# Four graph layers on one core: layer 1 folds W1 W2 ahead of the adjacency, the next pair's norm (in layer 3 its scores too) is issued half a pair ahead, attention weights are 1024 nodes wide

## Chip, core and metric

The kernel runs on one core of one Trainium2 chip. The metric is device time in microseconds (us). "Ratio" always means the mean time of one kernel's fast runs over that of the other's in the same rounds, with a 95% interval, so it is not quite the ratio of the two medians that are quoted.

## The reference, cut to what matters

x is [8, 2048, 64] in fp32, adj is [2048, 2048]. Each of four layers is `x = x + layer(relu(layernorm(x)))`.

```python
# layer 0: T0 = h, T1 = A h, T2 = 2 A (A h) - h; weights per node, w_n = sum_d embedding[n,d] weight[d]
# layer 1
v = h with row 0 replaced by intervention_value
for _ in range(3):
    effects = adj @ v                                  # per batch
    v = relu([v, effects] @ W1.T + b1) @ W2.T + b2
# layer 2: adj @ h, a scale and bias per channel, a linear map
# layer 3: graph attention
e   = leaky_relu(s1[:, None] + s2[None, :], 0.2)       # s1 = h @ a1, s2 = h @ a2
att = softmax(where(adj > 0.5, e, -9e15))
out = elu(att @ h)
```

## The kernel before

Two batches (a "pair") are worked on at a time, so every layer has four pairs. adj lies transposed in SBUF for the whole run. A product with it takes node-major data (128 nodes by 16 chunks by 128 channels) as the stationary operand and gives blocks of 512 nodes, feature-major. The tile framework gives each tile a buffer in program order ("two `blkb` tiles" means that the third waits until the first has been read), and then a scheduler sets the order on each engine. In the traces a ready instruction waits behind the one ahead of it in that order: in the kernel before, a weight on VectorE, for which TensorE then waited 0.75 us, began at 2306.29 us, behind an elu operation that had waited 1.26 us for GpSimd (both rows stand in the prediction).

The norm ahead of each layer. Its squares lie in `blkb`.

```python
    def norm_relu(xt, name):
        h = node_tile(f"h_{name}")
        mean = small.tile([P, G2], F32, name="mean")
        nc.vector.tensor_reduce(mean, groups(xt), axis=AX.X, op=ALU.add)
        ...                                             # h = x - mean
        for q in range(4):
            sq = blk("blkb", f"sq_{name}_{q}")
            nc.scalar.activation(sq, h[:, 4 * q:4 * q + 4, :]..., AF.Square)
            nc.vector.tensor_reduce(var[:, 8 * q:8 * q + 8], sq..., axis=AX.X, op=ALU.add)
        ...
        nc.gpsimd.tensor_tensor(rstd, var, mhalf, op=ALU.pow)
        nc.vector.scalar_tensor_tensor(groups(h), groups(h), 0.0, spread(rstd, C), op0=ALU.max, op1=ALU.mult)
```

Layer 1, the step that is done 3 times 4 blocks for each pair.

```python
                ps = adj_mm(v, nb, f"1_{p}_{s}")                     # 16 matmuls of 512
                eT = blk("blka", f"eT_{nm}")
                nc.vector.tensor_copy(eT, ps)
                ph = bank("tr", f"ph_{nm}")
                nc.tensor.matmul(ph, later["w1v"], vT[:, cols], start=True, stop=False)
                nc.tensor.matmul(ph, later["w1e"], eT, start=False, stop=True)
                hT = blk("blkb", f"hT_{nm}")
                nc.scalar.activation(hT, ph, AF.Relu, bias=later["b1"])
                pn = back_to_nodes(hT, later["w2"], nm)              # 4 matmuls of 128: "bn"
                ...
                if not last:
                    nc.vector.tensor_tensor(v_new[:, js, :], pn, ..., op=ALU.add)
                    pv = bank("tr", f"pv_{nm}")
                    nc.tensor.matmul(pv, later["w2"], hT, start=True, stop=True)
                    nc.scalar.activation(vT[:, cols], pv, AF.Identity, bias=later["b2"])
```

Layer 3 for each pair: scores with their products on VectorE, then per batch and block of 512 nodes 16 weights and 16 products on TensorE; then the elu, partly on GpSimd.

```python
                for j in range(NCH):
                    w = l3p.tile([P, 512], F32, name="w", bufs=3)
                    nc.vector.scalar_tensor_tensor(w, Grow[:, nb * 512:(nb + 1) * 512], R[:, j, bb:bb + 1],
                                                   adjT[nb][:, j, :], op0=ALU.max, op1=ALU.mult)
                    nc.tensor.matmul(acc[:C + 1, :], he[:, j, :], w, start=(j == 0), stop=(j == NCH - 1))
```

The loop around it issues a pair's norm when the pair begins:

```python
        for p in range(NP):
            xt = x_next
            h = norm_relu(xt, f"{layer}_{p}")
            ...
            attention(p, xt, h, l3p, ones)
```

Of the kernel before, what the change touches and what calls it, by code (L numbers as in the profile page):

```python
# [18 lines left out]
# Exponent shifts of the attention weights, see attention().  # L19
# [4 lines left out]
def kernel(  # L24
# [19 lines left out]
    """Four residual layers over one graph, two batches ("a pair") at a time.  # L44

    Two layouts of a pair's [node, batch, channel] values are used:
    node-major    [128 nodes, 16 node chunks, 2 batches x 64 channels] and
    feature-major [2 batches x 64 channels, 2048 nodes].
    adj is transposed once and stays in SBUF; a product with it takes a node-major
    operand (stationary) and gives a feature-major result.  # L50
    """
# [17 lines left out]
    adjT = [adjp.tile([P, NCH, 512], F32, name=f"adjT{nb}") for nb in range(NB)]  # L69
# [48 lines left out]
    def norm_relu(xt, name):  # L118
        """relu(layernorm(x)), node-major; mean and variance over each node's 64 channels."""
        h = node_tile(f"h_{name}")  # L120
# [3 lines left out]
        nc.vector.tensor_tensor(groups(h), groups(xt), spread(mean, C), op=ALU.subtract)  # L124
        var = small.tile([P, G2], F32, name="var")
        for q in range(4):
            sq = blk("blkb", f"sq_{name}_{q}")
            nc.scalar.activation(sq, h[:, 4 * q:4 * q + 4, :].rearrange("p j f -> p (j f)"), AF.Square)
            nc.vector.tensor_reduce(
                var[:, 8 * q:8 * q + 8], sq.rearrange("p (g c) -> p g c", c=C), axis=AX.X, op=ALU.add  # L130
            )
# [4 lines left out]
            groups(h), groups(h), 0.0, spread(rstd, C), op0=ALU.max, op1=ALU.mult  # L136
# [3 lines left out]
    def adj_mm(v, nb, name):  # L140
        """[2 x 64 channels, 512 nodes] of adj @ v, in PSUM."""
        ps = bank("mm", f"av_{name}_{nb}")
        for m in range(NCH):
            nc.tensor.matmul(ps, v[:, m, :], adjT[nb][:, m, :], start=(m == 0), stop=(m == NCH - 1))  # L144
        return ps
# [20 lines left out]
    def load_adj(nb):  # L166
        for t in range(4):
            r0 = nb * 512 + t * P
            for q in range(4):
# [5 lines left out]
                dst = adjT[nb][:, 4 * q:4 * q + 4, t * P:(t + 1) * P]  # L175
# [8 lines left out]
    # L0 weights, [input channel (on both partition halves), k, (d, output channel)]  # L184
# [7 lines left out]
    # embedding @ bias, node-major  # L192
# [17 lines left out]
    def two_halves(src, width, name):  # L210
        t = consts.tile([P, width], F32, name=name)
        for hf in range(2):
            nc.sync.dma_start(t[hf * C:(hf + 1) * C, :], src)
        return t

    def row(src, reps, name):
        """64 values of a DRAM vector, `reps` times over, on every partition."""
        t = consts.tile([P, reps, C], F32, name=name)
        nc.sync.dma_start(t, bass.AP(tensor=src.tensor, offset=src.offset, ap=[[0, P], [0, reps], [1, C]]))
        return t  # L220

    def block_diag_T(src, name):
        """[[src.T, 0], [0, src.T]] of a [64, 64] DRAM matrix."""
# [5 lines left out]
        t = consts.tile([P, P], F32, name=name)  # L229
# [8 lines left out]
    def load_later():  # L238
# [3 lines left out]
        later["wo"] = block_diag_T(w_out, "wod")  # L242
        later["b1"] = two_halves(b1[:, None], 1, "b1c")
        later["b2"] = two_halves(b2[:, None], 1, "b2c")
        later["bnl"] = two_halves(b_nl[:, None], 1, "bnl")
        later["b2r"] = row(b2, 2, "b2r")
        later["bor"] = row(b_out, 2, "bor")
        later["a1"] = row(a[:C, 0], 1, "a1r")
        later["a2"] = row(a[C:, 0], 1, "a2r")
        wn = two_halves(w_nl, 2, "wnl")  # L250
        ws = consts.tile([P, 1], F32, name="wsum")
        nc.vector.tensor_scalar(wn, wn, INV_SQRT2, None, op0=ALU.mult)
        nc.vector.tensor_tensor(ws, wn[:, 0:1], wn[:, 1:2], op=ALU.add)
        later["wsum"] = ws
# [6 lines left out]
    def layer0(p, xt, h):  # L261
# [23 lines left out]
        for nb in range(NB):  # L285
            ps = adj_mm(t1, nb, f"{nm}b")
            t2T = blk("blka", f"t2T_{p}_{nb}")
            nc.vector.scalar_tensor_tensor(  # L288
                t2T, ps, 2.0, t0T[:, nb * 512:(nb + 1) * 512], op0=ALU.mult, op1=ALU.subtract
            )  # L290
# [21 lines left out]
    def back_to_nodes(fT, wmat, name):  # L312
        """fT [2 x 64, 512 nodes] through a block-diagonal weight: node-major, in PSUM."""
# [12 lines left out]
    def layer1(p, xt, v):  # L326
        steps = 3
        nc.scalar.copy(v[0:1, 0, :], later["iv"])
        vT = to_feat(v, f"1_{p}")
        add_row(xt, later["b2r"])  # L330
        for s in range(steps):
            last = s == steps - 1
            v_new = None if last else node_tile(f"v_{p}_{s}")
            for nb in range(NB):
                nm = f"1_{p}_{s}_{nb}"
                cols = slice(nb * 512, (nb + 1) * 512)
                ps = adj_mm(v, nb, f"1_{p}_{s}")
                eT = blk("blka", f"eT_{nm}")
                nc.vector.tensor_copy(eT, ps)  # L339
                ph = bank("tr", f"ph_{nm}")  # L340
                nc.tensor.matmul(ph, later["w1v"], vT[:, cols], start=True, stop=False)  # L341
                nc.tensor.matmul(ph, later["w1e"], eT, start=False, stop=True)  # L342
                hT = blk("blkb", f"hT_{nm}")
                nc.scalar.activation(hT, ph, AF.Relu, bias=later["b1"])  # L344
                pn = back_to_nodes(hT, later["w2"], nm)
# [3 lines left out]
                else:  # L349
                    f = later["b2r"].rearrange("p b c -> p (b c)")  # L350
                    nc.vector.tensor_tensor(
                        v_new[:, js, :], pn, f[:, None, :].to_broadcast([P, 4, 2 * C]), op=ALU.add
                    )
                    pv = bank("tr", f"pv_{nm}")
                    nc.tensor.matmul(pv, later["w2"], hT, start=True, stop=True)
                    nc.scalar.activation(vT[:, cols], pv, AF.Identity, bias=later["b2"])
            v = v_new

# [1 line left out]
    def layer2(p, xt, h):  # L360
        add_row(xt, later["bor"])
        for nb in range(NB):
            ps = adj_mm(h, nb, f"2_{p}")
            gT = blk("blka", f"gT_{p}_{nb}")
# [5 lines left out]
    def make_mask():  # L370
        for nb in range(NB):
            for q in range(4):
                m = adjT[nb][:, 4 * q:4 * q + 4, :]
                nc.vector.tensor_scalar(m, m, THRESHOLD, None, op0=ALU.is_gt)

# [1 line left out]
    # With z = s1_i + s2_j, exp(leaky_relu(z)) = max(exp(z), exp(0.2 z))  # L377
    #   = exp(0.2 s1_i) exp(s2_j) max(exp(0.8 s1_i), exp(-0.8 s2_j)),
    # and the factor of i alone cancels in the softmax. With S = max_j s2_j, the three factors
    # are scaled to  # L380
    #   e_j = exp(s2_j - S + QE), G_i = exp(0.8 (s1_i + S) - KR), R_j = exp(0.8 (S - s2_j) - KR).
    # G_i is capped at exp(CAP): above every R_j it is a factor of i alone again. All stay in
    # range for any s1 and for S - s2_j up to 132; |h| <= 8 after the layer norm bounds it by
    # 8 sqrt(2) |a2|.
    # A row without neighbours is a softmax over equal values: the mean of all h_j.
    def attention(p, xt, h, l3p, ones):
        s1 = l3p.tile([P, NCH, 2], F32, name="s1", bufs=1)
        s2 = l3p.tile([P, NCH, 2], F32, name="s2", bufs=1)
        for s, ar in ((s1, later["a1"]), (s2, later["a2"])):
            flat = s.rearrange("p j b -> p (j b)")  # L390
            for q in range(4):
                tmp = blk("blkb", f"hs_{p}_{q}")
                tg = tmp.rearrange("p (g c) -> p g c", c=C)
                nc.vector.tensor_tensor(
                    tg, groups(h)[:, 8 * q:8 * q + 8, :], ar.to_broadcast([P, 8, C]), op=ALU.mult
                )
                nc.vector.tensor_reduce(flat[:, 8 * q:8 * q + 8], tg, axis=AX.X, op=ALU.add)
        # S of each batch, on every partition
# [13 lines left out]
        G = l3p.tile([P, NCH, 2], F32, name="G", bufs=1)  # L412
# [7 lines left out]
        # sum of h over the nodes, on every partition  # L420
        pS = bank("tr", f"pS_{p}")
        for j in range(NCH):
            nc.tensor.matmul(pS[:, :2 * C], ones, h[:, j, :], start=(j == 0), stop=(j == NCH - 1))
        hsum = l3p.tile([P, 2 * C], F32, name="hsum", bufs=1)
        nc.vector.tensor_copy(hsum, pS[:, :2 * C])

        for bb in range(2):
            bs = slice(bb * C, (bb + 1) * C)
            Grow = feat_tile(f"Grow_{p}_{bb}")
            for nb in range(NB):  # L430
                pg = bank("tr", f"pg_{p}_{bb}_{nb}")
                for t in range(4):
                    nc.tensor.transpose(
                        pg[:, t * P:(t + 1) * P],
                        G[:, 4 * nb + t, bb:bb + 1].to_broadcast([P, P]), ident,
                    )
                nc.scalar.copy(Grow[:, nb * 512:(nb + 1) * 512], pg)  # L437
            he = l3p.tile([P, NCH, C + 1], F32, name="he")
            nc.vector.tensor_tensor(
                he[:, :, :C], h[:, :, bs], E[:, :, bb:bb + 1].to_broadcast([P, NCH, C]), op=ALU.mult  # L440
            )
            nc.scalar.copy(he[:, :, C:], E[:, :, bb:bb + 1])
            for nb in range(NB):
                nm = f"{p}_{bb}_{nb}"
                acc = bank("mm", f"acc_{nm}")
                for j in range(NCH):
                    w = l3p.tile([P, 512], F32, name="w", bufs=3)
# [96 lines left out]
```

## Time and profile before

| before | |
|---|---|
| time | 2748.63 us median of 3 runs (2747.21 to 2751.48) |
| layer 0, 1, 2, 3 | 979, 896, 243, 627 us |
| TensorE idle in them | 97, 48, 2, 120 us |
| TensorE busy, whole run | 90% of the span |

The lengths are cut at the layers' first products in the trace.

### The profile page before, as it was taken

The numbers are of one execution on the slowest core, as the hardware profiler recorded it, in microseconds if no ns is written. First come the engines' busy times: TensorE is split into PE (matmuls) and PEld (weight loads), VectorE is DVE, ScalarE is ACT, GpSimd is POOL, SyncE is SP. The second block draws the span as 40 slices with busy tenths as digits, with TensorE's granted clock in tenths as the row PEclk, the third lists the DMA queues.
The fourth block names the chain that finished last, engine by engine and source line by source line (L and its number), as shares of the span: only waits on it lengthen the run. The fifth ranks groups of instructions, "written<-read, shape, count | busy, mean of one in ns | idle before, by whom it ended". The sixth has DMA issues, their size and how long they took to land.

```text
span 2745.0 us, 18187 instructions
## 1 busy us (share of the span) xinstructions
PE 2478.4 (90%) x7296; PEld 1075.3 (39%) x7296; DVE 1160.1 (42%) x2245; ACT 219.2 (8%) x393; POOL 177.7 (6%) x138
## 2 busy tenths in 40 slices
PE   5889999999999999989989989998999977959697
PEld 3444444443443444434434434443444223222232
DVE  3135626626526530110110111012227878878787
ACT  1110010010000000010010000001001110111110
POOL 0000000000000000000000000001000120111111
PEclk7999999999999999999999999999999998979899
DMA  6310000010000000000000000000001010000000
GB/s 135 123 48 1 19 13 1 1 31 1 0 31 1 0 31 0 0 31 0 0 31 0 0 22 9 0 0 31 31 31 61 2 30 1 8 23 8 8 1 16
DMA packets 40873, 53.55 MB, mean 20 GB/s; under 512 B 28500, under 2 KB 28500, under 8 KB 37716
## 3 DMA queue, kind: packets, MB, share of 16 engines
q1 hardware_dynamic: 37908, 35.60, 4.5%
q0 software_dynamic: 2880, 16.78, 1.8%
q8 instruction: 58, 0.95, 0.1%
q14 instruction: 27, 0.22, 0.0%
HBM read 35.59 MB, written 16.78 MB: 19 GB/s over the span
## 4 chain that ended last, share of the span: by engine, by line
PE 57%; issue 23%; DVE 13%; POOL 5%; ACT 1%; DMA 1%; SPq 0%; POOLq 0%; DVEq 0%; ACTq 0%
PE av L144 32%; DVE x L307 10%; PE y L300 3%; PE bn L316 3%; POOL rstd L134 2%; PE av_2a L144 2%; PE av_3a L144 2%; PE av_1a L144 2%; PE ph L342 2%; PE av_3b L144 2%; PE av_2b L144 2%; PE av_1b L144 2%; PE av_0b L144 2%; PE ph L341 2%; POOL yx L476 1%
## 5 line engine op out<-in xcount | busy, mean ns | idle before, releaser
L452 PE MATMUL acc<-w,he 128*65 128x512 f32 x1024 | 459.8, 597 | 21.4 <-DVE w L448 21.0
L144 PE MATMUL av<-adjT,h 128*128 128x512 f32 x1024 | 452.2, 598 | 11.0 <-DVE h L135 11.0
L144 PE MATMUL av<-adjT,v 128*128 128x512 f32 x1024 | 449.9, 592 | 0.0
L448 DVE SCALAR_TENSOR_TENSOR w<-Grow,R,adjT 128x512 f32<-128x512 f32 x512 | 380.2, 758 | 37.4 <-ACT Grow L437 12.0
L307 DVE SCALAR_TENSOR_TENSOR x<-y,emb,x 128x128 f32<-128x128 f32 x1024 | 355.0, 350 | 69.8 <-PE y L300 31.0
L144 PEld LDWEIGHTS av<-adjT,h 128*128 128x128 f32 x1024 | 195.3, 192 | 249.3 <-issue 238.1
L339 DVE COPY eT<-av 128x512 f32<-128x512 f32 x48 | 33.2, 692 | 607.9 <-PE av L144 607.9
L144 PEld LDWEIGHTS av<-adjT,v 128*128 128x128 f32 x1024 | 193.6, 190 | 239.2 <-issue 239.2
L452 PEld LDWEIGHTS acc<-w,he 128*65 128x65 f32 x1024 | 129.0, 137 | 323.1 <-DVE w L448 208.8
L300 PE MATMUL y<-wt,T 64*128 64x512 f32 x512 | 144.2, 635 | 35.9 <-DVE x L307 32.3
L300 PE MATMUL y<-wt,t2T 64*128 64x512 f32 x512 | 135.2, 594 | 8.9 <-DVE t2T L288 8.9
L300 PE MATMUL y<-wt,t1T 64*128 64x512 f32 x512 | 134.4, 591 | 0.0
L134 POOL TENSOR_TENSOR rstd<-var,mhalf 128x32 f32<-128x32 f32 x16 | 87.2, 5451 | 454.1 <-DVE var L132 453.9
L105 POOL DMA_DIRECT2D xs<-x x12 | 7.2, 602 | 1586.5 <-DVE x L348 859.8
L300 PEld LDWEIGHTS y<-wt,T 64*128 64x128 f32 x512 | 43.3, 187 | 132.4 <-PE y L300 104.2
L275 DVE COPY t<-t 128x512 f32<-128x512 f32 x16 | 11.1, 691 | 195.3 <-PE t L274 195.3
L344 ACT ACTIVATE hT<-ph,b1c 128x512 f32<-128x512 f32 x48 | 33.0, 687 | 707.2 <-PE ph L342 693.0
L300 PEld LDWEIGHTS y<-wt,t2T 64*128 64x128 f32 x512 | 55.1, 188 | 65.0 <-issue 53.4
L174 PE MATMUL adjt<-ident,adj 128*128 128x128 f32 x256 | 48.3, 334 | 33.6 <-DMA adj<-in_adj_dram 31.7
L300 PEld LDWEIGHTS y<-wt,t1T 64*128 64x128 f32 x512 | 55.5, 188 | 55.6 <-issue 55.6
L135 DVE SCALAR_TENSOR_TENSOR h<-h,rstd 128x2048 f32<-128x2048 f32 x16 | 36.7, 2292 | 89.9 <-POOL rstd L134 89.9
L402 PE MATMUL pm<-ident,mx 128*2 128x128 f32 x4 | 1.4, 346 | 78.4 <-DVE mx L400 78.4
(134 smaller groups left out, 1823.0 us busy)
## 6 DMA issues: line engine op xcount, KB each, us to landing
adj<-in_adj_dram SPq DMA_DIRECT2D x64, 256.0 KB, 3.7
xs<-x POOLq DMA_DIRECT2D x12, 1024.0 KB, 4.2
x<-xs SPq DMA_DIRECT2D x12, 1024.0 KB, 4.8
x<-in_x_dram SPq DMA_DIRECT2D x8, 512.0 KB, 6.5
out_dram<-x POOLq DMA_DIRECT2D x8, 512.0 KB, 4.8
wt<-in_L_gnn_weight_dram SPq DMA_DIRECT2D x6, 256.0 KB, 6.8
emb<-in_L_gnn_embedding_dram SPq DMA_DIRECT2D x1, 128.0 KB, 5.7
b2r<-in_L_gnn_b_dram SPq DMA_DIRECT2D x1, 64.0 KB, 5.6
```

What stands on the lines that cost most here:

```text
L134: nc.gpsimd.tensor_tensor(rstd, var, mhalf, op=ALU.pow)
L135: nc.vector.scalar_tensor_tensor(groups(h), groups(h), 0.0, spread(rstd, C), op0=ALU.max, op1=ALU.mult)
L144: nc.tensor.matmul(ps, v[:, m, :], adjT[nb][:, m, :], start=(m == 0), stop=(m == NCH - 1))
L174: nc.tensor.transpose(ps[:, m * P:(m + 1) * P], st[:, m * P:(m + 1) * P], ident)
L300: nc.tensor.matmul(y[:, bb, :], terms[k][hs, :], wt[hs, k, dg * 512:(dg + 1) * 512], start=(k == 0), stop=(k == K - 1),)
L307: nc.vector.scalar_tensor_tensor(xj, y[:, :, d * C:(d + 1) * C], emb[:, j, e:e + 1], xj, op0=ALU.mult, op1=ALU.add,)
L316: nc.tensor.matmul(ps[:, t, :], fT[:, t * P:(t + 1) * P], wmat, start=True, stop=True)
L339: nc.vector.tensor_copy(eT, ps)
L341: nc.tensor.matmul(ph, later["w1v"], vT[:, cols], start=True, stop=False)
L342: nc.tensor.matmul(ph, later["w1e"], eT, start=False, stop=True)
L448: nc.vector.scalar_tensor_tensor(w, Grow[:, nb * 512:(nb + 1) * 512], R[:, j, bb:bb + 1], adjT[nb][:, j, :], op0=ALU.max, op1=ALU.mult,)
L452: nc.tensor.matmul(acc[:C + 1, :], he[:, j, :], w, start=(j == 0), stop=(j == NCH - 1))
```

## The change

Its intent: fewer matmuls in layer 1; norms and scores hidden behind the pair before; fewer VectorE instructions in layer 3. `hook()` issues the next pair's norm, and in layer 3 its scores too; in layers 0 to 2 it stands at the second of a pair's four blocks (layer 2's is cut here). The diff, cut to its core:

```diff
 # layer 1: u = W1e v goes through adj, W1 W2 is one matrix, relu's result in a feature tile
+        for nb in range(NB):
+            pn = back_to_nodes(gT[:, nb * 512:(nb + 1) * 512], later["w1e"], f"u_{p}_{nb}")
+            nc.vector.tensor_copy(u[:, 4 * nb:4 * nb + 4, :], pn)
...
-                ps = adj_mm(v, nb, f"1_{p}_{s}")
-                eT = blk("blka", f"eT_{nm}")
-                nc.vector.tensor_copy(eT, ps)
-                ...                                         # ph: two matmuls
-                hT = blk("blkb", f"hT_{nm}")
-                nc.scalar.activation(hT, ph, AF.Relu, bias=later["b1"])
-                pn = back_to_nodes(hT, later["w2"], nm)
+                nc.tensor.matmul(ps, later["w1v2" if s else "w1v"], gT[:, cols], start=True, stop=False)
+                for m in range(NCH):
+                    nc.tensor.matmul(ps, u[:, m, :], adjT[:, nb, m, :], start=False, stop=(m == NCH - 1))
+                nc.scalar.activation(gT_new[:, cols], ps, AF.Relu, bias=later["b1s" if s else "b1"])
+                if last and nb == 1:
+                    hook()                                  # the next pair's norm
+                pn = back_to_nodes(gT_new[:, cols], later["w2" if last else "w1e2"], nm)
-                    pv = bank("tr", f"pv_{nm}")             # and its copy
 # layer 0: T2's factor and difference go into the weights
-            nc.vector.scalar_tensor_tensor(t2T, ps, 2.0, t0T[...], op0=ALU.mult, op1=ALU.subtract)
+            nc.scalar.copy(t2T, ps)
+            if nb == 1:
+                hook()
 # layer 3: weights of 1024, score products on GpSimd, elu's -1 taken from x beforehand
-                nc.vector.tensor_tensor(tg, groups(h)[:, 8 * q:8 * q + 8, :], ar..., op=ALU.mult)
+                nc.gpsimd.tensor_tensor(tg, hg[:, 8 * q:8 * q + 8, :], ar..., op=ALU.mult)
...
+        nc.gpsimd.tensor_scalar(xt, xt, -1.0, None, op0=ALU.add)
...
+                    w = w2j[:, j % 2]                       # two tiles of two weights: four in all
+                    nc.vector.scalar_tensor_tensor(w, Grow, R[:, j, bb:bb + 1],
+                                                   adjT[:, 2 * n2:2 * n2 + 2, j, :], op0=ALU.max, op1=ALU.mult)
+                    for t in range(2):
+                        nc.tensor.matmul(acc[:C + 1, t, :], h[:, j, bb, :], w[:, t, :], ...)
+                    if bb == 0 and n2 == 1 and j == 0:
+                        hook()                              # the next pair's norm and scores
```

A "half" below is one batch and 1024 nodes in layer 3: 32 products on TensorE, four halves to a pair. The second half of a pair carries the hook.

## The prediction

> **What bounds the kernel now.** I read the busy time per stretch first, cut at the layer boundaries that the chain of waits shows, then the groups by shape, the chain of waits inside layer 1, and two stretches of the timeline. The first view gives, for each layer, its length and then the busy time of TensorE, weight loads, VectorE, ScalarE and GpSimd, the granted clock and the DMA.
>
> ```profile
> 0.00:979.00 979.00, 882.51 (x3002) 403.20 (x3003) 462.75 (x1156) 50.57 (x86) 29.89 (x14) 0.97 0.10 28
> 979.00:1875.00 896.00, 847.65 (x2236) 386.94 (x2234) 116.51 (x145) 74.21 (x115) 24.73 (x9) 0.97 0.03 12
> 1875.00:2118.00 243.00, 241.47 (x641) 111.50 (x641) 84.13 (x89) 21.96 (x32) 23.57 (x7) 0.99 0.07 26
> 2118.00:2745.00 627.00, 506.73 (x1421) 173.67 (x1419) 496.67 (x858) 72.42 (x160) 99.55 (x108) 0.92 0.05 14
> ```
>
> TensorE is busy 95% of layer 1 and 99% of layer 2: there only fewer matmuls or a shorter gap helps. In layer 3 it idles 120 us while VectorE is busy 79%: neither is full, so they wait for each other. Layer 0 idles 97 us, mostly while adj loads and where VectorE works off the per-node sums.
>
> The chain inside layer 1 (start, us, what) gives the period of one 512-node block in steps 1 and 2, 17.64 us:
>
> ```profile
> 1047.76 1.05 PE ph L342 x2
> 1049.67 1.14 PE bn L316 x8
> 1050.81 0.86 PE pv L355 x2
> 1051.66 12.88 PE av L144 x30
> ```
>
> An fp32 matmul is two instructions; 30 in 12.88 us make 0.858 us per matmul of 512 columns. The block is 18 of them (16 of adj, two of W1), a "bn" of 1.16 us, and "pv", 0.86. The last step has no pv and takes 16.78.
>
> At a pair's end the timeline shows what TensorE waits for:
>
> ```profile
> 1417.20 5.45 POOL L134 TENSOR_TENSOR rstd<-var,mhalf 128x32 f32<-128x32 f32 x1 [1.58 <-DVE var L132]
> 1422.69 2.29 DVE L135 SCALAR_TENSOR_TENSOR h<-h,rstd 128x2048 f32<-128x2048 f32 x1 [5.64 <-POOL rstd L134]
> 1425.37 3.76 PE L152 MATMUL tf<-ident,h 128*128 128x128 f32 x16 [11.36 <-ACT h L328]
> ```
>
> The norm of the next pair ends in the open: 11.4 us idle, and a pair comes every 225 us. In layer 2, and at most pairs of layer 0, the norm is already under matmuls.
>
> Layer 3 has blocks of 15.3 us (8 per pair) and, once per pair, a gap: pairs repeat every 162 us, 8 x 15.3 = 122.5 of them blocks. The gap is norm, scores and weights in a row on VectorE:
>
> ```profile
> 2262.52 2.29 DVE L135 SCALAR_TENSOR_TENSOR h<-h,rstd 128x2048 f32<-128x2048 f32 x1 [5.58 <-POOL rstd L134]
> 2264.85 1.29 DVE L394 TENSOR_TENSOR hs<-h,a1r 128x512 f32<-128x512 f32 x2
> 2274.42 2.27 DVE L122 TENSOR_REDUCE mean<-x 128x32 f32<-128x2048 f32 x1
> 2280.97 2.36 DVE L439 TENSOR_TENSOR he<-h,E 128x1024 f32<-128x1024 f32 x2
> 2286.76 13.22 DVE L448 SCALAR_TENSOR_TENSOR w<-Grow,R,adjT 128x512 f32<-128x512 f32 x16 [0.76 <-ACT Grow L437]
> 2303.91 0.91 DVE L448 SCALAR_TENSOR_TENSOR w<-Grow,R,adjT 128x512 f32<-128x512 f32 x1
> 2304.35 1.01 POOL L476 TENSOR_TENSOR yx<-yx,o 128x256 f32<-128x256 f32 x1
> 2306.08 0.29 DVE L479 TENSOR_SCALAR yx<-yx 128x256 f32<-128x256 f32 x1 [1.26 <-POOL yx L477]
> 2306.29 0.75 DVE L448 SCALAR_TENSOR_TENSOR w<-Grow,R,adjT 128x512 f32<-128x512 f32 x1
> ```
>
> The last four rows show the wait that will matter: the next weight stands behind an elu operation that waits for GpSimd.
>
> [...] (692 for N=512; he, 1222 for 1024), and the weight in the groups view is 758, somewhat over. Back to back, starts are closer than durations: 0.66 us for a weight of 512 (2306.29 to 2306.95). So I take 1.2 us for one of 1024. [...] the GpSimd add beside a weight took 1.01 us, without one 0.69, and that weight 0.91 instead of 0.75. [...]
>
> **Layer 1.** Since v = W2 g + b2, the change sends u = W1e v through adj and folds W1 W2. One pass then needs 16 adj matmuls and one more in the same PSUM bank; the copy eT, the second W1 matmul and pv go. A block becomes 17 x 0.858 + 1.16 = 15.75, plus about 0.1: in the order of instructions one 0.86 matmul covers the relu (0.69 plus latency, 0.95). 48 x 15.85 = 761. Each pair adds to_feat 3.76 and u = W1e v, four times 1.16 = 4.64: 8.4, with a small wait 9, so 36. Its norm is issued in the last step and the order shows it finished under matmuls. Sum 797 for 896: **-99**, less 2 where VectorE still drains layer 0's sums: -97.
>
> **Layer 0.** T2 is folded into the weights; t2T becomes a ScalarE copy, and no longer stands behind the norm on VectorE. Before, TensorE waited for it 2.96 us in pairs 1 to 3 (8.9 in all). The per-node sums stay: 0.384 us each (61 in 23.42 us), 3.07 per tile of 8, above TensorE's 2.85. **-8**. The two operations on wt (about 2 us) fall where VectorE is idle.
>
> **Layer 2.** The same matmuls, no gap to close: 0.
>
> **Layer 3.** TensorE per half (1024 nodes, one batch): 32 x 0.858 = 27.4 plus transposes of the result 1.2. VectorE: 16 weights x 1.2 = 19.2 instead of 32 x 0.66 = 21.1, and the elu loses two operations. So a half is bound by TensorE once started. But the order puts both blocks' elu in one run on VectorE, behind four weights (two tiles are all the buffers). Six GpSimd operations (0.61 to 0.7, 4.6 us in all) and two exps stand in it. Counting from the end of the half before: weights 2 and 3 by 2.5 us, divisor by 4, GpSimd by 7, elu by 8.4, weight 4 by 9.7; TensorE has used up four by 8.1. It loses 1.6: **30.3 per half**. Where the transposes of G stand behind the half before (second half of the next pairs, and third) no weight is ahead; the first comes at 4.9 and the second at 10.3, then 15 x 1.72: **36**.
>
> The half that carries the next pair's norm and scores: weights alternate with this work. VectorE in order waits for squares (their two buffers are the elu's too), then for the power, 5.45 us with one weight in it[...]. [...] My count: second weight at 10, fifth at 17, sixth at 25, tenth at 40, eleventh at 41; then on TensorE the sum of h, 3.84, and the last six weights, 10.3: **56**, 52 in pair 0, where four weights are ahead.
>
> Pair 0: 29 + 52.5 + 36 + 30.3 = 148. Pairs 1 and 2: 30.3 + 56 + 36 + 30.3 = 152.6. Pair 3: 30.3 + 36 + 30.3 + 30.3 = 127. With 8 at the start (scores half hidden already) and 17 from the last matmul to the stored output: 605 for 627, **-22**. A gap of some 40 us turns into three slow halves.
>
> **Sum.** -97 - 8 - 22 = -127; 2748.6 - 127 = 2621 us, 4.6% faster.
>
> **Rivals.** (a) The half-pair lead hides everything in layer 3. For it: VectorE's own work per pair, 77 of weights and some 32 else, is below TensorE's 124. Then layer 3 is 16 x 28.6 + 18.6 of G transposes + 15.4 of sums + 25 = 517 at the least, and the kernel 2533[...]. (b) GpSimd becomes the bound: if the power[...], the products and the subtraction of 1[...] block weights for their full length, each hooked pair costs 8 to 10 more: layer 3 unchanged, 2645. (c) Layer 1's gap only moves: relu and u in sequence at step boundaries. The last chunk of u is needed 12 matmuls in, so I expect nothing; a wait of 2 us per boundary would add 24. Against it: before, step boundaries cost the same 17.64.
>
> **Range.** Layer 1 is counted matmuls, good to 8 us; layer 3 could go from -60 to about 0. Predicted 2621, range 2580 to 2655. Faster by over 2% (below 2694) 0.96; within 2% 0.035; slower 0.005.
>
> **What would show it.** Layer 1: blocks of 15.8 to 15.9, pairs every 200, no idle before tf above 1 us; above 16.5 breaks the step. Layer 0: no wait for t2T. Layer 3: weights of 1024 near 1.25 us; halves of about 30, 36 and 56;[...] TensorE's waits concentrated before weights in the second half of pairs 0 to 2. If hooked halves take under 40, rival (a) is nearer and the time nearer 2580; if plain halves exceed 33, VectorE's order costs more than I count.

## More of the kernel before

TensorE is nearly full in layers 1 and 2, so what costs there is a matmul more, or a gap. In layer 3 neither TensorE nor VectorE is full (507 and 497 of 627 us). The lines that show this stand in the prediction. One thing to look for in them later is who uses which buffer: ScalarE computed the four squares of the next pair only behind the pair's last relu:

```profile
1412.10 0.69 ACT L344 ACTIVATE hT<-ph,b1c 128x512 f32<-128x512 f32 x1 [16.10 <-PE ph L342]
1412.69 0.62 ACT L128 ACTIVATE sq<-h 128x512 f32<-128x512 f32 x1
```

The relu's result `hT` lies in `blkb` too.

## The result

The kernel after takes 2592.78 us (median of 4 runs, 2591.69 to 2597.24) beside 2749.52 us of before (4 runs). The ratio is 0.9432, interval 0.9419 to 0.9446. The prediction was 2621 us with a range of 2580 to 2655.

Busy time by layer, kernel after, cut as before (columns: stretch, its length, busy us of TensorE, its weight loads, VectorE, ScalarE and GpSimd with their instruction counts, granted TensorE clock, DMA share, GB/s):

```profile
0.00:976.00 976.00, 881.13 (x3006) 401.57 (x3007) 453.56 (x1141) 59.77 (x102) 29.91 (x14) 0.97 0.10 28
976.00:1754.00 778.00, 776.36 (x2205) 370.39 (x2204) 94.41 (x117) 51.81 (x83) 24.20 (x8) 1.00 0.03 11
1754.00:1992.00 238.00, 237.11 (x638) 109.53 (x636) 82.97 (x80) 21.52 (x32) 41.38 (x17) 1.00 0.10 36
1992.00:2589.80 597.80, 507.58 (x1427) 178.47 (x1427) 429.90 (x512) 69.24 (x157) 149.93 (x135) 0.96 0.05 14
```

| us | before | after | difference | predicted |
|---|---|---|---|---|
| layer 0 | 979 | 976 | -3 | -8 |
| layer 1 | 896 | 778 | -118 | -97 |
| layer 2 | 243 | 238 | -5 | 0 |
| layer 3 | 627 | 597.8 | -29 | -22 |
| sum | 2745 | 2589.8 | -155 | -127 |

In layer 1 TensorE is now busy 776 of 778 us: no gap is left. The start of a pair, in the timeline, answers to the 11.36 us wait of before; the transposes of the next pair begin in front of the last "bn" of the pair, and no wait stands behind them:

```profile
1169.73 0.93 PE L158 MATMUL tf<-ident,h 128*128 128x128 f32 x7
1170.67 1.16 PE L347 MATMUL bn<-w2d,gT 128*128 128x128 f32 x8
1176.68 1.02 PE L376 MATMUL av<-T,w1v 128*128 128x512 f32 x2
```

There was a cost in the old gaps that the idle time does not show. In the kernel before, the window behind a gap has TensorE fully busy, but its granted clock (the third number from the end) is half:

```profile
1425.30:1429.00 3.70, 3.63 (x17) 3.27 (x18) 2.06 (x2) 1.77 (x4) 0.00 (x0) 0.50 0.00 0
...
1875.13 17.82 PE L144 MATMUL av<-adjT,h 128*128 128x512 f32 x34 [11.03 <-DVE h L135]
```

The clock was 1.00 again from 1430.6 us. The second line is the start of layer 2: 34 instructions took 17.82 us, where 34 of 0.43 us (0.858 for a matmul of two) are 14.6; the granted clock was 0.50 from 1875 to 1881 us and 1.00 from 1884. So 3.2 us of layer 2's 5 were the gap at the end of layer 1, paid in layer 2.

In layer 3 the hooked half is the slow one. Timeline of the kernel after, second half of pair 1 (from 2177.0 to 2233.2 us; taken from ScalarE's copies of the finished sums):

```profile
2175.20 5.37 POOL L477 TENSOR_SCALAR x<-x 128x2048 f32<-128x2048 f32 x1 [18.85 <-DVE h L130]
2183.14 3.68 PE L503 MATMUL acc<-w,h 128*65 128x512 f32 x4 [4.54 <-DVE w L497]
...
2192.82 6.44 POOL L140 TENSOR_TENSOR rstd<-var,mhalf 128x32 f32<-128x32 f32 x1 [7.41 <-DVE var L138]
2202.84 1.97 PE L503 MATMUL acc<-w,h 128*65 128x512 f32 x2 [5.73 <-DVE w L497]
2205.59 1.58 DVE L497 SCALAR_TENSOR_TENSOR w<-Grow,R,adjT 128x1024 f32<-128x1024 f32 x1
```

TensorE waits 4.54 us for a weight at the start and 5.73 behind the power; from there on, weights come one by one among reductions of GpSimd's products. The lengths of all halves, from one such copy to the next:

| half | pair 0 | pair 1 | pair 2 | pair 3 | predicted |
|---|---|---|---|---|---|
| second (hooked in pairs 0 to 2) | 48.9 | 56.1 | 56.2 | 35.4 | 52, 56, 56, 36 |
| third | 37.0 | 37.0 | 35.3 | 29.8 | 36, 36, 36, 30.3 |
| other | 29.8 | 29.8 | 29.8 | 29.8 | 30.3 |

Layer 0 holds three waits in place of the old three of 2.96 us. TensorE waits 1.98 us for VectorE in pairs 1 and 2 (pair 1 is shown), and 3.16 in pair 3 for a copy on ScalarE:

```profile
412.83 1.14 PE L331 MATMUL y<-wt,T 64*128 64x512 f32 x4 [1.98 <-DVE x L338]
...
837.65 2.08 PE L331 MATMUL y<-wt,t2T 64*128 64x512 f32 x4 [3.16 <-ACT t2T L319]
```

### The profile page after: what moved, and what is told of

Read it like the earlier page. It is cut to its first block, busy times and chain, and to the rows that moved or that the text cites. A ratio compares the mean times of both kernels' runs of the same rounds, so it can differ in the third digit from the quotient of the medians.

```text
span 2589.8 us, 17869 instructions
## 1 busy us (share of the span) xinstructions
PE 2402.2 (93%) x7272; PEld 1060.0 (41%) x7272; DVE 1060.8 (41%) x1848; ACT 202.3 (8%) x373; POOL 245.4 (9%) x174
## 4 chain that ended last, share of the span: by engine, by line
PE 67%; DVE 17%; issue 9%; POOL 5%; ACT 1%; DMA 1%; SPq 0%; POOLq 0%; DVEq 0%; ACTq 0%
PE av L380 24%; PE acc L503 12%; DVE x L338 10%; PE av L150 8%; PE y L331 4%; PE bn L347 3%; POOL rstd L140 2%; DVE w L497 2%; PE av_3a L150 2%; PE av_2a L150 2%; PE av_1a L150 2%; PE av_2b L150 2%; PE av_3b L150 2%; PE av_1b L150 2%; PE av_0b L150 2%
## 5 line engine op out<-in xcount | busy, mean ns | idle before, releaser
L380 PE MATMUL av<-adjT,u 128*128 128x512 f32 x1536 | 667.1, 592 | 0.0
L503 PE MATMUL acc<-w,h 128*65 128x512 f32 x1024 | 466.1, 609 | 73.9 <-DVE w L497 73.6
L380 PEld LDWEIGHTS av<-adjT,u 128*128 128x128 f32 x1536 | 288.4, 190 | 345.8 <-issue 344.6
L497 DVE SCALAR_TENSOR_TENSOR w<-Grow,R,adjT 128x1024 f32<-128x1024 f32 x256 | 324.4, 1306 | 60.1 <-PE acc L503 59.3
L503 PEld LDWEIGHTS acc<-w,h 128*65 128x65 f32 x1024 | 138.8, 141 | 375.7 <-issue 238.3
L150 PE MATMUL av<-adjT,h 128*128 128x512 f32 x512 | 222.5, 592 | 0.0
L393 DVE TENSOR_TENSOR u<-bn,r1e 128x512 f32<-128x512 f32 x32 | 22.1, 691 | 392.6 <-PE bn L347 392.6
L150 PEld LDWEIGHTS av<-adjT,h 128*128 128x128 f32 x512 | 96.1, 190 | 114.8 <-issue 114.8
L391 DVE TENSOR_TENSOR x<-bn,x 128x512 f32<-128x512 f32 x16 | 11.1, 692 | 188.0 <-PE bn L347 188.0
L180 PE MATMUL adjt<-ident,adj 128*128 128x128 f32 x256 | 44.3, 306 | 35.5 <-DMA adj<-in_adj_dram 33.2
L150 PE MATMUL av_0a<-adjT,h 128*128 128x512 f32 x128 | 58.8, 615 | 13.0 <-DVE h L141 12.9
```

Source lines behind the costliest of these rows:

```text
L150: nc.tensor.matmul(ps, v[:, m, :], adjT[:, nb, m, :], start=(m == 0), stop=(m == NCH - 1))
L180: nc.tensor.transpose(ps[:, m * P:(m + 1) * P], st[:, m * P:(m + 1) * P], ident)
L380: nc.tensor.matmul(ps, u[:, m, :], adjT[:, nb, m, :], start=False, stop=(m == NCH - 1))
L393: nc.vector.tensor_tensor(u_new[:, js, :], pn, later["r1e"][:, None, :].to_broadcast([P, 4, P]), op=ALU.add,)
L497: nc.vector.scalar_tensor_tensor(w, Grow, R[:, j, bb:bb + 1], adjT[:, 2 * n2:2 * n2 + 2, j, :], op0=ALU.max, op1=ALU.mult,)
L503: nc.tensor.matmul(acc[:C + 1, t, :], h[:, j, bb, :], w[:, t, :], start=(j == 0), stop=(j == NCH - 1),)
```

## The experiments

My theory after the result: in layer 1 fold and lead each give about half, in layer 3 the lead trades three gaps for three slow halves. The main rival was that one of the two does it all. All outputs are right.

### Layer 1 without its lead

```diff
         elif layer == 1:
-            layer1(p, xt, h, hook)
+            layer1(p, xt, h, lambda: None)
+            hook()
```

> The kernel after, but in layer 1 the norm of the next pair is issued behind the pair instead of half a pair ahead, so that layer 1 has the fold without the lead. My theory: the gap of 11 us before each pair comes back (four times, the last before layer 2), and with it the slow clock behind it: 4 x (11.4 + 0.8 idle + 2 to 3 at half clock) = 57 to 61 us over the kernel after, about 2650; blocks inside a pair stay at 15.7. Rival, my prediction's view that a gap costs only its idle time: 4 x 11.4 = 46 over, about 2638. Rival two, the lead is worth nothing because TensorE's queue is behind anyway: within 10 of after.

Measured: 2595.44 us, ratio to before 0.9439 (0.9425 to 0.9454), where the kernel after has 0.9432 (0.9419 to 0.9446). My theory fell: taking the lead out of layer 1 costs nothing. In the order of instructions the scheduler had moved the norm back under the last products by itself; the first transposes of the next pair still stand ahead of the last "bn". The traces show how little the place of issue did: in both kernels the norm's power starts 57.9 us ahead of the pair's store (1309.33 and 1367.27 us in the kernel after, 1311.94 and 1369.88 here).

### Layer 1 without the fold, lead kept

The layer 1 of before stands in the kernel after, with the hook at the same place:

```diff
-                nc.tensor.matmul(ps, later["w1v2" if s else "w1v"], gT[:, cols], start=True, stop=False)
...
+                ps = adj_mm(v, nb, f"1_{p}_{s}")
+                ...                                         # eT, ph, hT in blkb, pv: as before
+                if last and nb == 1:
+                    hook()
```

> The kernel after, but with the unfolded layer 1 of the kernel before; the norm of the next pair is still issued half a pair ahead. My theory: blocks of 17.64 and 16.78 us come back, less the extra W1 product at the start of a pair; per pair 12 blocks with one matmul more (12 x 0.858) and 8 with a second more (8 x 0.858), less four bn of u (4.0): 13.2, so 4 x 13.2 = 53 over after, about 2646. With the run without the lead this should add up: 53 + 59 against the 118 that layer 1 fell. Rival: fold and lead work on the same gap and each alone gives nearly all; then this run is within 25 of after.

Measured: 2659.97 us, ratio 0.9673 (0.9658 to 0.9687). That is 67 us over the kernel after, not 53. By the trace layer 1 is 841 us here, 63 over, of which I had counted 53: a block of the first two steps is 17.64 us again, 1.97 over 15.67, where I had taken two matmuls, 1.72; the rest lies ahead of layer 1, where this kernel is the same. So the fold is worth 63 and the lead, without the fold, 55; but the run before this one says that with the fold the lead is worth nothing. Something in the fold does the lead's work too.

### Fillers for a gap that was not there

To try the clock, 120 transposes of the identity were set ahead of pairs 1 to 3, in the kernel without the lead:

```diff
+        if p:
+            for r in range(2):
+                warm = bank("tr", f"warm_{p}_{r}")
+                for q in range(60):
+                    nc.tensor.transpose(warm[:, (q % 4) * P:(q % 4 + 1) * P], ident, ident)
```

> As the fold alone in layer 1 (no lead), but 120 transposes of the identity into two spare banks stand ahead of the transposes of pairs 1, 2 and 3, to keep TensorE busy in the gap. They need no data and depend on nothing but the two banks. My theory: the clock falls to about half in an 11 us gap and needs some us of work to come back; with the fillers the first work of a pair runs at full clock, and the run is 1.5 to 3 us per pair faster than the fold alone, 5 to 9 us in all. Rival: the slow first matmuls are waits for operands, not the clock; then it is the same as the fold alone, or slower by what the fillers overrun the gap.

Measured: 2636.0 us, ratio 0.9588 (0.9572 to 0.9604), 40.6 over the kernel without the lead. The run was submitted together with that one, on the belief that it has gaps; it has none, so 3 times 13.3 us of fillers (the pairs come every 207.7 instead of 194.4 us) came on top. It says nothing of the clock.

### The squares made to wait

What else did the fold change? The relu's result left `blkb`, the two buffers that the squares need. This run puts only that back, for the last step:

```diff
+                gT_b = blk("blkb", f"hT_{nm}") if last else gT_new[:, cols]
-                nc.scalar.activation(gT_new[:, cols], ps, AF.Relu, ...)
+                nc.scalar.activation(gT_b, ps, AF.Relu, ...)
...
-                pn = back_to_nodes(gT_new[:, cols], later["w2" if last else "w1e2"], nm)
+                pn = back_to_nodes(gT_b, later["w2" if last else "w1e2"], nm)
```

> The fold without the lead came out level with the kernel after, so layer 1 needs no lead in the program. My new theory: the gap of before came from a buffer. There the relu's result hT of every block lay in the two tiles that the norm's squares also take, so the squares of the next pair could not begin before the last blocks had been read; the fold put the relu's result into a feature tile and set the squares free. This run is the fold without the lead, with only the relu's results of the last step put back into those two tiles. Buffer theory: the gap of 11.4 us before every pair is back, with the slow clock behind it: 4 x (11.4 + 2 to 4) = 54 to 62 over the fold alone, about 2650 to 2657. Rival: something else in the fold (fewer steps on VectorE, its order) hides the norm; then within 5 of the fold alone.

Measured: 2651.7 us, ratio 0.9643 (0.9627 to 0.9659): 56.3 over the fold alone, in the expected range. The gap is back, and to the hundredth the one of before:

```profile
1393.16 3.76 PE L158 MATMUL tf<-ident,h 128*128 128x128 f32 x16 [11.36 <-ACT h L361]
```

Layer 1 in the runs that give a table, one line from each trace: lead without fold, then fold without lead, then fold with the squares waiting (cut at the first transposes of layer 1 and the first adj product of layer 2):

```profile
982.00:1823.00 841.00, 839.32 (x2238) 381.47 (x2235) 117.76 (x150) 73.80 (x115) 24.19 (x8) 1.00 0.03 11
```

```profile
978.00:1756.00 778.00, 776.37 (x2206) 370.18 (x2202) 94.82 (x119) 51.67 (x83) 24.19 (x8) 1.00 0.03 11
```

```profile
978.00:1809.00 831.00, 781.94 (x2211) 375.55 (x2208) 95.30 (x120) 52.42 (x83) 24.73 (x9) 0.97 0.03 13
```

| layer 1, us | no lead | lead |
|---|---|---|
| no fold, relu in the squares' buffers | 896 | 841 |
| fold, relu in the squares' buffers | 831 | not run |
| fold, relu in its own tile | 778 | 778 |

Read it down: the fold's matmuls are worth 63 to 65 us. The gap is worth 53 to 55, and either the lead or the freed buffers closes it. The lead helps where the squares share buffers because it puts them, in program order, ahead of the last relus; where the buffers are free the scheduler does not need the help. The idle part is three gaps of 11.36 us and one of 11.03, 45 us; the last "bn" of a pair, no longer covered, waits 0.84 us more, 3.4 in all. What is left, 4.5 to 6.5 us, is 1.5 to 2.2 us for each of the three gaps that have work of layer 1 behind them; the next run asks whether that is the slow clock.

### The gap filled

```diff
+                for q in range(45):                         # ... as above, 2 x 45, with the squares waiting
+                    nc.tensor.transpose(warm[:, (q % 4) * P:(q % 4 + 1) * P], ident, ident)
```

> As the run with the squares waiting, plus 90 transposes of the identity (some 9.6 us) in each of the gaps before pairs 1, 2 and 3; the order of instructions shows them between the last products of a pair and the next pair's first transposes. Clock theory: the granted clock no longer falls in these three gaps, and the run is 3 x (2 to 4) = 6 to 12 us faster than the one with the squares waiting. Rival, the slow start is a wait for operands: level with it (within 2), or slower by what the fillers overrun.

Measured: 2649.2 us, ratio 0.9633 (0.9619 to 0.9648), 2.5 us faster than with the squares waiting: the sign of the clock theory, a fraction of its size, and at this spread of the runs not a difference to rest on. The trace tells why it is so little, and more. The fillers ended 2.3 us before the next transposes could start. Behind that wait the clock was 0.60 in pair 2 all the same, but 1.00 in pair 1. Pairs 1 and 2, first the transposes, then the window behind the wait (clock third from the end):

```profile
1184.64 1.09 PE L158 MATMUL tf<-ident,h 128*128 128x128 f32 x8 [2.31 <-ACT h L366]
...
1391.32 2.48 PE L158 MATMUL tf<-ident,h 128*128 128x128 f32 x12 [2.30 <-ACT h L366]
```

```profile
1185.00:1189.00 4.00, 3.76 (x32) 3.38 (x31) 2.34 (x4) 2.25 (x4) 0.00 (x0) 1.00 0.00 0
1391.00:1395.00 4.00, 3.68 (x19) 3.46 (x20) 2.13 (x1) 2.02 (x4) 0.00 (x0) 0.60 0.00 0
```

So these two starts compare the clock within one run. From the first transpose to the first adj product pair 1 took 6.9 us and pair 2 took 8.2 for the same instructions (pair 3, whose clock is not shown here, took 8.3): behind this wait the slow clock cost 1.3 us. In the run without fillers the stretch is 9.1 to 9.3 us, with one more W1 product (0.86) ahead of the adj product, so behind a full gap (clock 0.50 from 1393 to 1397 us there) the slow clock cost 1.3 to 1.5 us by the same comparison.

### Layer 3 without its lead

```diff
-            attention(p, xt, h, l3p, *sc, hook)
+            attention(p, xt, h, l3p, *sc, lambda: None)
+            hook()
```

> The kernel after, but in layer 3 norm and scores of the next pair are issued behind the pair instead of inside its second half. My theory: the three hooked halves (49, 56, 56) fall to about 36, which gives back 53, and three gaps of 34 to 40 us between pairs come in: 102 to 120. Sum +50 to +67, about 2645 to 2660, layer 3 some 650. Rival, that the lead only moves the gap: layer 3 within 10 of after, about 2590 to 2600. Rival two, that the lead hides everything: +100 or more.

Measured: 2643.47 us, ratio 0.9613 (0.9599 to 0.9627), 50.7 over the kernel after, at the low edge of my theory. From a pair's first finished sum to the next pair's it takes 167, 167 and 164 us, against 146, 153 and 151 with the lead and 161, 163 and 158 before the change. So without its lead, layer 3 of the changed kernel is some 5 us a pair slower than the old one. The trace shows two likely causes in the open gap, neither tested alone: the score products come from GpSimd at 1.15 us each, and small operations on VectorE wait beside the subtraction of 1. This one has 32 elements in a row and took 2.72 us, where its neighbour took 0.18:

```profile
2161.49 5.37 POOL L477 TENSOR_SCALAR x<-x 128x2048 f32<-128x2048 f32 x1 [4.95 <-DVE h L130]
...
2162.45 2.72 DVE L453 TENSOR_TENSOR s<-s,S 128x32 f32<-128x32 f32 x1
```

### Weights 512 wide again

```diff
-                    nc.vector.scalar_tensor_tensor(w, Grow, R[:, j, bb:bb + 1], adjT[:, 2 * n2:2 * n2 + 2, j, :], ...)
+                    for t in range(2):
+                        nc.vector.scalar_tensor_tensor(w[:, t, :], Grow[:, t, :], R[:, j, bb:bb + 1],
+                                                       adjT[:, 2 * n2 + t, j, :], ...)
```

> The kernel after with each attention weight of 1024 made by two operations of 512 instead of one. 256 weights become 512 operations: 0.66 x 2 - 1.2 = 0.12 us more each on VectorE, 31 us in all. My theory: plain halves are bound by TensorE and keep 29.8, only halves where VectorE is the limit (hooked, and where no weight is ahead) grow: 0 to +12. Rival, the width is what made layer 3 faster: +25 to +31.

Measured: 2589.17 us, ratio 0.9416 (0.9402 to 0.9430), so not slower than the kernel after; the intervals overlap. The groups view, kernel after and then this run (busy us, mean ns of one, idle before them):

```profile
L497 DVE SCALAR_TENSOR_TENSOR w<-Grow,R,adjT 128x1024 f32<-128x1024 f32 x256 | 324.4, 1306 | 60.1 <-PE acc L503 59.3 <-issue 0.7
```

```profile
L498 DVE SCALAR_TENSOR_TENSOR w<-Grow,R,adjT 128x512 f32<-128x512 f32 x512 | 372.2, 781 | 54.6 <-PE acc L504 36.9 <-ACT Grow L489 17.7
```

VectorE works 48 us more and the kernel pays nothing. Hooked halves grew by 1 to 4 us, but the third halves fell from 37 to 33.8 and pair 3's second from 35.4 to 30.5. The width of the weights, one of the three parts of the change by name, brings no time of its own.

### Score products back on VectorE

```diff
-                nc.gpsimd.tensor_tensor(
+                nc.vector.tensor_tensor(
                     tg, hg[:, 8 * q:8 * q + 8, :], ar.to_broadcast([P, 8, C]), op=ALU.mult
```

> The kernel after with the eight score products of a pair (128x512) on VectorE again, as before the change, 0.69 us each instead of 1.6 on GpSimd beside weights. Contention theory: in the hooked halves VectorE gets 5.5 us more work, but weights no longer stretch (a weight beside two products took up to 3 us in the staged run, 1.27 alone) and no reduction waits for GpSimd: -3 to -8 per hooked half, -10 to -25 in all. Rival, the move to GpSimd was a gain because VectorE is the hooked half's limit: +5 x 3 = +15 to +17.

Measured: 2610.94 us, ratio 0.9492 (0.9479 to 0.9505), 18 slower: the contention theory missed here, and the rival (+15 to +17) came close. Hooked halves are 54.2, 60.1 and 62.6. In this order all eight products and eight reductions stand in one block on VectorE (2212.9 to 2222.4 us in the trace) with no weight between, and TensorE waits behind it:

```profile
2223.74 1.97 PE L503 MATMUL acc<-w,h 128*65 128x512 f32 x2 [7.07 <-DVE w L497]
```

On GpSimd the products (1.6 us each in the kernel after) had come slowly enough for the scheduler to set weights between. So this run compares two orders as much as two engines, and the last pair of runs puts the question again.

### A staged lead

The next pair's norm and scores become a generator that is advanced between weights: mean, squares, norm, each product, each at its own weight of the pair; and the transposes of G for the next half come in the middle of the current one.

```diff
-                    if bb == 0 and n2 == 1 and j == 0:
-                        hook()
+                    if j == 4 and (bb, n2) != (1, 1):
+                        Gr = grow(*((bb, 1) if n2 == 0 else (1, 0)))
+                    hook(32 * bb + 16 * n2 + j)             # next piece, if due
```

> The kernel after, but the next pair's norm and scores in layer 3 are issued a piece at a time over the whole pair, each between two weights, and the transposes of G of the next half in the middle of the current one. My theory: the hooked halves and the halves behind G lose because this work stands in one run between weights with four weights of buffer; spread out, a half costs TensorE's own 29.8 to 32, and layer 3 falls by 40 to 75, to 2520 to 2553. Rival, contention with GpSimd's products or the single power stretches weights wherever they lie: within 15 of after.

Measured: 2578.71 us, ratio 0.9379 (0.9365 to 0.9393): 14 faster than the kernel after, inside the rival's 15 and far from the 40 to 75 that I expected. Pair 1 takes 146.7 us (halves of 41.9, 34.2, 34.1 and 36.5) for 152.7. The trace shows the pieces spread out as meant, and weights stretched beside GpSimd. Here two of them took 4.66 us beside the subtraction of 1, where two alone take 2.48:

```profile
2169.65 6.33 POOL L522 TENSOR_SCALAR x<-x 128x2048 f32<-128x2048 f32 x1 [16.30 <-DVE h L487]
...
2171.86 4.66 DVE L548 SCALAR_TENSOR_TENSOR w<-Grow,R,adjT 128x1024 f32<-128x1024 f32 x2
```

### Staged, and off GpSimd

```diff
-                nc.gpsimd.tensor_tensor(tg, hg[...], ar..., op=ALU.mult)
+                nc.vector.tensor_tensor(tg, hg[...], ar..., op=ALU.mult)
-        nc.gpsimd.tensor_scalar(xt, xt, -1.0, None, op0=ALU.add)
+        nc.scalar.activation(xt, xt, AF.Identity, bias=neg1)
+        box["Gr"] = grow_of(p, box["sc"][0], l3p, 0, 0)     # next pair's first G, in this pair's last half
-        nc.scalar.copy(v[0:1, 0, :], later["iv"])           # layer 1
+        nc.gpsimd.tensor_copy(v[0:1, 0, :], later["iv"])
```

> The staged lead with five more things: the score products on VectorE, the subtraction of 1 from x on ScalarE, the transposes of G for the next pair's first half issued in this pair's last half, the stages moved a few weights, and layer 1's intervention row copied by GpSimd. Contention theory: the 4 to 12 us that the halves of the staged run lie above 29.8 are weights stretched beside GpSimd (two weights 4.66 beside the subtraction, 3.71 and 4.31 beside products) plus 5 for G at the start of a pair; without them a pair of three costs TensorE's 119 + 3.8 + some 6: 130 to 136 for 147, and the kernel falls by 30 to 50, to 2530 to 2550. Rival, VectorE's own work (some 114 us a pair) with four weights of buffer is the limit: within 12 of the staged run.

Measured: 2530.47 us (2529.49 to 2531.49, 4 runs), ratio to before 0.9204 (0.9191 to 0.9217). It beats both kernels: 8.0% less than before, and by the medians 62 us less than after. Layer 3 of its trace:

```profile
1990.00:2528.40 538.40, 492.98 (x1431) 174.49 (x1429) 434.44 (x536) 76.27 (x160) 102.00 (x108) 0.99 0.06 16
```

A pair takes 132 us, with halves of 33.8, 33.2, 34.3 and 30.7. Where no norm is in the way (pair 3) three of the halves are 30.7: the 29.8 of TensorE's own work and 1.0 of transposes of G. Moving the intervention row off ScalarE also did what the wait in layer 0 had asked for: from that place in pair 3 to the end of layer 0 it takes 140.0 us instead of 143.1. But five things were changed at once, so two were taken back one at a time.

### One thing taken back: the products

```diff
-                nc.vector.tensor_tensor(tg, hg[...], ar..., op=ALU.mult)
+                nc.gpsimd.tensor_tensor(tg, hg[...], ar..., op=ALU.mult)
```

> The staged version off GpSimd with one thing taken back: the score products on GpSimd again. It frees VectorE of 5.5 us of products a pair and sets eight GpSimd products beside weights. Contention theory: a weight beside a product is stretched from 1.27 to 1.8 to 3 us, as in the first staged run; eight products of some 1.3 to 2 us stretch six or more weights by about 1 each, about the 5.5 saved: within 6 of the run before, on either side. If VectorE's own work is the limit: -6 to -12. If contention dominates: +6 to +15.

Measured: 2542.74 us, ratio 0.9243 (0.9231 to 0.9256), 12.3 slower: contention dominates. The weights' mean rises from 1283 to 1351 ns, 17 us over 256 of them, which is more than the 15.9 us of products that VectorE was spared; and each product takes 1.86 us on GpSimd against 0.68 on VectorE. It is not a wait for the products: VectorE's idle time behind them is 0.5 us in all. A product and the two weights beside it (2.48 us if alone):

```profile
2214.15 3.39 DVE L555 SCALAR_TENSOR_TENSOR w<-Grow,R,adjT 128x1024 f32<-128x1024 f32 x2
2214.32 2.14 POOL L514 TENSOR_TENSOR hs<-h,a1r 128x512 f32<-128x512 f32 x1 [0.61 <-DVE s L517]
```

### The other thing taken back: the subtraction of 1

```diff
-        nc.scalar.activation(xt, xt, AF.Identity, bias=neg1)
+        nc.gpsimd.tensor_scalar(xt, xt, -1.0, None, op0=ALU.add)
```

> The staged version off GpSimd with one thing taken back: the subtraction of 1 from x (128x2048) on GpSimd again instead of ScalarE. Contention theory: GpSimd holds for 5.4 to 6.3 us and the weights beside it for up to 3.4 each; three pairs of 3 to 4 us, and the power of the same pair starts behind it: +8 to +15. Rival: it lies where weights are ahead and costs nothing: within 3.

Measured: 2542.16 us, ratio 0.9245 (0.9232 to 0.9257), 11.7 slower, as the contention theory had it. One weight beside the subtraction took 3.47 us, where a weight alone takes 1.27; and the variances that the norm's power needs stand on VectorE behind that weight:

```profile
2157.01 6.33 POOL L538 TENSOR_SCALAR x<-x 128x2048 f32<-128x2048 f32 x1 [15.54 <-DVE h L489]
2159.21 3.47 DVE L555 SCALAR_TENSOR_TENSOR w<-Grow,R,adjT 128x1024 f32<-128x1024 f32 x1
```

In both of these runs VectorE's order of some weights and reductions moved as well, so engine and order are not wholly told apart. Of the 48 us between the first staged run and the best one, the two things, each taken back alone, account for 24 if they add up (not run together), and the intervention row for 3. The other 21 lie between the earlier transposes of G (pair 3, which has no norm to carry: first half 35.4 to 30.7) and the moved stages, which were not told apart.

### Tried without a run

Three kernels that put the power on VectorE, to take GpSimd's 5.45 us out of the chain, could not be built, nor could the fold alone in the kernel before, which is why both halves of the table above were made from the kernel after.

## Why the prediction was right, and where it was off

**Layer 1, -97 predicted, -118 measured.** The matmul count held: 17 for 18 and no pv. Two terms were mis-sized and one reason was wrong. (1) A block was put at 15.85 us and measures 15.67: "bn" was counted with its whole 1.16 us, but it takes 1.0 until the next group starts, while the relu's 0.1 came as 0.08. Over 48 blocks that is 9 us. (2) The start of a pair was put at 9 us and measures 6.4 (194.42 a pair less twelve blocks): I took 3.76 for the transposes from the kernel before, where they ran at half clock (0.50) behind a gap. In the kernel after the sixteen are 2.3 us (128 in 18.2), at a clock of 1.00 in the start shown above. Over four pairs that is 10. (3) The allowance of 2 us for VectorE's drain did not show. Together 21. The step that failed as a reason is "its norm is issued in the last step and the order shows it finished under matmuls". It does finish there, but with the fold not because of where it is issued: the run without the lead has the same time, and without the lead the gap comes back only when the squares' buffers are taken away as well. Lead and freed buffers each close the gap; the prediction saw only the lead. Rival (c), a gap that only moves, is out: the blocks across step boundaries take 15.73 and 16.05 us.

**Layer 0, -8 predicted, -3 measured.** "Before, TensorE waited for it 2.96 us in pairs 1 to 3" was right, and in pairs 1 and 2 that wait went, but others took its place: 1.98 us for VectorE's sums in pairs 1 and 2, in pair 1 with half clock behind it (0.50 from 415 to 417 us), and in pair 3 a wait of 3.16 us for the same t2T. The three sum to 7.1 us, where 8.9 stood before. There ScalarE's list has the copy of the intervention row, which needs the next norm, ahead of t2T: the adj product that t2T copies ended at 832.5 us, the row's copy began at 836.82 and t2T's at 837.02. The profile of before could not show that; the order of the changed kernel would have, had I read ScalarE's as well.

**Layer 2, 0 predicted, -5 measured.** 3.2 of it is the slow clock at its start (0.50 from 1875 to 1881 us), which belongs to layer 1's last gap. I had read idle time as the whole price of a gap.

**Layer 3, -22 predicted, -29 measured.** The mechanism held: three gaps became three slow halves, of 48.9, 56.1 and 56.2 for 52, 56 and 56. What was too long was the plain half (29.8 for 30.3), pair 0's hooked half, and the tail (14 us for 17). The 162 us that the prediction read for a pair of before is 158 to 163 by the copies of the sums. Rival (a), all hidden at 517 us, was far off, but as a bound it was useful: the best version comes to 538. Rival (b), GpSimd as the bound, was wrong as a total and right in its direction. Weights ran longer beside GpSimd's long operations (3.47 us for 1.27 beside the subtraction, two in 3.39 for 2.48 beside a product), and each of the two cases that were tested alone cost 12 us. The count had this partly inside, with times for the products that were the author's estimate and not read from a trace; in the kernel after, the hooked half's weights came every 3.26 us among the products (2205.59, 2208.85, 2212.11 us), and a product took 1.6 us.

**The weights of 1024.** I counted 19.2 us of weights in a half instead of 21.1 and claimed no time for it, since a half is TensorE's. The run at 512 agrees.

## What to carry to other kernels

Before crediting a gap to where a thing is issued, look at which buffers it needs and who else holds them: here a result moved to other buffers was worth as much as issuing half a pair ahead. Spread hidden work between the instructions it competes with, rather than issue it in one run, and keep long GpSimd operations away from VectorE instructions such as these weights (12 us in each of two runs here). Halving the number of weight instructions on an engine that is not the bound was worth nothing here, and it took one run to find out.

## What the traces showed of the clock and of GpSimd

- The length of a wait alone did not decide the granted clock behind it. Of the two waits of 1.98 us in layer 0 of the kernel after, the first was followed by a granted clock of 0.50 (pair 1, window below), the second by 1.00 (pair 2, 628 to 631 us). Of two waits of 2.3 us in the gap-filled run, the first was followed by 1.00 (pair 1), the second by 0.60 (pair 2). Behind the 11.36 us gap of the kernel before, which ended at 1425.37 us, it was 0.50 until 1430.5 us and 1.00 from 1430.6.

```profile
415.00:417.00 2.00, 2.00 (x6) 0.80 (x4) 0.77 (x3) 0.00 (x0) 0.00 (x0) 0.50 0.03 8
```

- The subtraction of 1 over 128x2048 took 5.37 us on GpSimd in the kernel after, 6.33 beside weights in the staged run; the same on ScalarE took 1.99, and VectorE's operations of 2048 take 2.3.
- A weight of 1024 went from 1.27 to 3.47 us beside the subtraction, and two weights from 2.48 to 3.39 beside a product of 512. The weight of 3.47 us began 2.2 us after GpSimd's instruction did and ended 0.7 before it, so it was not held up to its end (times on GpSimd are rough).
- The power on GpSimd took 5.45 us for 32 elements on each partition, 6.4 when a weight ran beside it.
